# Shared expert, second group: four chunks of all four tiles' down products first, the last chunk and the half chunk behind them

## The chip, the cores and the metric

The kernel runs on one core of a Trainium2 chip. The metric is the device time of one execution in microseconds (us); the median of several runs is compared.

## The reference

The program is one transformer block for 2 sequences of 1024 tokens of width 512, all in float32. Ahead of the part that matters here stand a modulation from a small matrix product, two layer norms, and an attention whose keys and values are summed over the sequence, so that each sequence has one mixed output matrix. Then a mixture of experts follows; every token has two of eight routed experts, and all tokens go through one shared expert:

```python
x = hidden_states.reshape(-1, d)
scores = softmax(x @ gate_w)
topk_w, topk_idx = top_k(scores, 2)
...
g = silu(einsum('td,edh->teh', x, w_gate)) * einsum('td,edh->teh', x, w_up)
routed = einsum('teh,ehd,te->td', g, w_down, comb)
shared = silu(x @ sw_gate) * (x @ sw_up) @ sw_down
out = routed + shared
```

The shared expert has a hidden width of 704: five chunks of 128 and a half chunk of 64. The block's result is the residual plus a gate row `gb` times `out`.

## The kernel before

The 2048 tokens are 16 tiles of 128, in four groups of four tiles (one group has 512 tokens). Group 0's shared expert is worked out during the attention. Group 1's comes right behind the routing, ahead of the routed experts; that is the place of the change. Groups 2 and 3 come at the very end.

**Hidden units of group 1.** For each of five chunks n, `seven` (L1105) makes seven products of half-size operands on the tensor engine (PE, L1123) into PSUM banks: m1 and m2 into one of the two `start` banks, m6 and m7 into an `out` bank, m5 and m3 (tile m53) into an `mm` bank, m4 into one of the two `tr` banks. The scalar engine (ACT) copies m1 (L1131), and the vector engine (DVE) adds the others one after the other: L1133 to L1135, L1138 (m5), L1139 (m3), L1140 (m4), L1141. ACT then takes the sigmoid into `gT[:, n, :]` (L1143) and DVE multiplies twice (L1144, L1145); with L1145 chunk n of gT is ready. The half chunk, number 5, was made ahead of the five by `half_up`; its even tiles lie in partitions 0 to 63 and its odd ones in 64 to 127, so that two products with it run on the two halves of the array at the same time. DVE also works out the tables of experts (`expert_tables`, behind chunk 2) and of rows (`choice_rows`, L893 to L907, behind chunk 4).

**Down products of group 1.** `shared_down` (L1023) multiplies, for each tile j0 to j3 of the group, the six pieces of gT (stationary) with the six pieces of the down weights (128x512, moving) and sums them in one PSUM bank (L1031, names `sd`). A 128x512 product in float32 stands as two records in the trace. `down_ps` hands the four tiles the banks tr, tr, start, start. The weights lie in tiles `wd_s0a` (chunks 0 to 2) and `wd_s1a` (chunks 3, 4 and the half). A scheduler orders each engine's instructions from priorities and dependences. On PE it put j0's chunks 0 to 3, then j1's chunk 0, then j0's chunk 4, and then j1's chunks 1 to 4 and the two half chunks; behind them j2's five chunks, j3's five and their half chunks.

**Eviction.** `keep_shared` (L1149) is called for two tiles at a time: DVE multiplies the bank with `gb` into a row of the room `spare` (L1153), and GpSimd (POOL) adds that row to the residual tile (L1154). `spare` has two rows in turn here.

**What follows: the first pair of blocks.** `pair_sums` makes four sums of the first pair's expert weights on DVE, in this order: L1609 (s1), L1611 (s3), L1610 (s2), L1612 (s4). They are placed by `tc.issue_after` behind j1's eviction. `pair_in` (L1574) transposes two tiles of gathered rows `hp` on PE (L344, `tr_p`) into the two `tr` banks, and ACT copies them to `hpT` (L1578). `Pair` makes four sums of these rows on DVE (L1594 to L1597) into the room `token_sums`, which is the same memory as `spare`. `pair_hidden` then makes seven products per pair on PE (L1629): m1 and m2 read `hpT` and weights alone, m6 reads token_sums (L1595) and s2, and the others follow. From there PE goes through nine pairs and the single blocks to the last groups of the shared expert.

**SP's queue** issues the loads: the rows and weights of the pairs (L1556, L976 to L982), and the first parts of the shared gate and up weights once more (`s_again`, L1441). The down weights of the second pair, `wd_p` (L978, L982), take the room of `wd_s0a` and wait until that was read for the last time.

```python
for _ in shared_down(1, gTs[1], wds, keep_shared, down_ps()):
    pass
...
with tc.issue_after(kept_shared[5].ins):
    for step in steps:
        step()
pair_of = {0: Pair(pair_in(0, hps.pop(0)), token_rooms[:, 0])}
```

Of the kernel before, what the change touches and what calls it, by code (L numbers as in the profile page):

```python
# [18 lines left out]
P = 128  # L19
# [5 lines left out]
def kernel(  # L25
# [20 lines left out]
    nc = tc.nc  # L46
    B, S, D = x.shape
    E, _, H = w_gate.shape
# [8 lines left out]
    NF = HS // P  # L57
    HP = P // 2
# [567 lines left out]
    rows = const.tile([P, NT, TOPK], I32, name="rows")  # L626
# [257 lines left out]
    def choice_rows():  # L884

        pk = picks.rearrange("p t s e -> p (t s) e")
        rf = rowf.rearrange("p t s -> p (t s)")

        room = Carved(choice_room[:, NT * TOPK * E :])

        def by_choice(v, name):
            prod = Carved(choice_room).tile([P, NT * TOPK, E], FP, name=f"prod_{name}")
            nc.vector.tensor_mul(prod, pk, v.unsqueeze(1).to_broadcast([P, NT * TOPK, E]))  # L893
            t = room.tile([P, NT * TOPK], FP, name=f"of_{name}")
            nc.vector.tensor_reduce(t, prod, AX.X, ALU.add)
            return t

        beyond = by_choice(choice_of["ends"], "ends")
        nc.vector.tensor_tensor(beyond, rf, beyond, ALU.is_ge)
        shift = by_choice(choice_of["by_pair"], "pair")  # L900
        other = by_choice(choice_of["by_block"], "block")
        nc.vector.tensor_scalar(other, other, float(Y0), None, ALU.add)
        nc.vector.tensor_sub(other, other, shift)
        nc.vector.tensor_mul(other, other, beyond)
        nc.vector.tensor_add(rf, rf, shift)
        nc.vector.tensor_add(rf, rf, other)
        nc.vector.tensor_copy(yrows.rearrange("p t s -> p (t s)"), rf)  # L907


    gTs = {}  # L910
# [21 lines left out]
    def shared_chunk(n, g, wt):  # L932

        if n == 0:
            gTs[g] = gtp.tile([P, NF + 1, 512], FP, tag="gT", name=f"gT_{g}")
        pss = []
        for i, w in enumerate(wt):
            ps = sh_ps(f"p{i}_{n}_{g}")
            for k in range(KC):
                nc.tensor.matmul(  # L940
                    ps, w[:, k, :], hT[g][:, k, :], start=(k == 0), stop=(k == KC - 1)
                )
            pss.append(ps)
        sgm = unit.tile([P, 512], FP, tag="sg", bufs=2, name=f"sg_{n}_{g}")
        if n < NF:
            gate_full(gTs[g][:, n, :], sgm, *pss)
        else:
            gate_half(gTs[g], sgm, pss[0])

    def chunk_weights(n):  # L950
        def fetch(w, c0, src, h0, m):
            nc.sync.dma_start(
                w[:, :, c0 : c0 + m],
                src[:, h0 : h0 + m].rearrange("(k p) h -> p k h", p=P),
            )

        a = unit.tile([P, KC, P], FP, tag="wg", bufs=2, name=f"cg_{n}")
        if n == NF:
            fetch(a, 0, sw_gate, n * P, HP)
            fetch(a, HP, sw_up, n * P, HP)  # L960
            return (a,)
        u = unit.tile([P, KC, P], FP, tag="wu", bufs=2, name=f"cu_{n}")
        fetch(a, 0, sw_gate, n * P, P)
        fetch(u, 0, sw_up, n * P, P)
        return a, u
# [37 lines left out]
    def shared_weights():  # L1003

        tiles = [weight_tiles(f"s{i}a") for i in range(2)]
        wgu = []
        for i, (wg, wu, wd) in enumerate(tiles):
            views = []
            for w, src in ((wg, sw_gate), (wu, sw_up)):
                v = w.rearrange("p k h -> p (k h)").rearrange("p (k h) -> p k h", k=KH)  # L1010
                nc.sync.dma_start(
                    v, src.rearrange("(k p) h -> p k h", p=P)[:, i * KH : (i + 1) * KH, :]
                )
                views.append(v)
            wgu.append(views)
        wds = load_down([wd for _, _, wd in tiles])

        def up_part(which, i, h0, m):
            return wgu[i][which][:, :, h0 : h0 + m]

        return up_part, wds

    def shared_down(g, gT, wds, use, ps_of, apart=False):  # L1023


        for j0 in range(0, 4, 2):
            pss = [ps_of(f"sd_{g}_{j0 + i}") for i in range(2)]

            def chunk(i, c):
                rows = slice(i * HP, (i + 1) * HP) if c == NF else slice(0, P)  # L1030
                nc.tensor.matmul(  # L1031
                    pss[i],
                    gT[rows, c, (j0 + i) * P : (j0 + i + 1) * P],
                    wds[c][rows, :],
                    start=(c == 0),
                    stop=(c == NF),
                )

            if apart and j0 == 2:
                for i in range(2):  # L1040
                    for c in range(NF + 1):
                        chunk(i, c)
            else:
                for i in range(2):
                    for c in range(NF):
                        chunk(i, c)
                    if i == 0:
                        yield
                for i in range(2):
                    chunk(i, NF)  # L1050
            for i in range(2):
                use(g * 4 + j0 + i, pss[i])
            yield
# [51 lines left out]
    def seven(n, g, weights, b, behind=None):  # L1105


        a11, a12, a22, s1, s2, s3, s4 = weights
        c1, c2 = (
            gpool.tile([P, 2 * TH], FP, tag="sg", bufs=8, name=f"c{i}_{n}_{g}")  # L1110
            for i in range(2)
        )
        (c11, c12), (c21, c22) = ((c[:, 0:TH], c[:, TH:]) for c in (c1, c2))

        def products(ps, *pairs):
            halves = []
            for i, (w, h) in enumerate(pairs):
                half = ps[:, i * TH : (i + 1) * TH]
                with ExitStack() as order:
                    if behind:  # L1120
                        order.enter_context(tc.issue_after(behind.ins))
                    for k in range(KH):
                        nc.tensor.matmul(  # L1123
                            half, w[:, k, :], h[:, k, :], start=(k == 0), stop=(k == KH - 1)
                        )
                halves.append(half)
            return halves

        add = nc.vector.tensor_add
        m1, m2 = products(start_ps(f"m12_{n}_{g}"), (a11, b.b11), (a12, b.b21))  # L1130
        nc.scalar.copy(c11, m1)  # L1131
        m6, m7 = products(out_ps(f"m67_{n}_{g}"), (s2, b.t2), (s3, b.t3))
        add(c12, c11, m6)  # L1133
        add(c11, c11, m2)
        add(c22, c12, m7)  # L1135
        m5, m3 = products(mm_ps(f"m53_{n}_{g}"), (s1, b.t1), (s4, b.b22))
        (m4,) = products(tr_ps(f"m4_{n}_{g}"), (a22, b.t4))
        add(c12, c12, m5)  # L1138
        add(c12, c12, m3)  # L1139
        add(c21, c22, m4)  # L1140
        add(c22, c22, m5)  # L1141
        dst = gTs[g][:, n, :]
        on_act = nc.scalar.activation(dst, c1, AF.Sigmoid)  # L1143
        nc.vector.tensor_mul(dst, dst, c1)  # L1144
        return on_act, nc.vector.tensor_mul(dst, dst, c2)  # L1145

    kept_shared = {}

    def keep_shared(t, ps):  # L1149
# [110 lines left out]
    def chunk(n):  # L1260
        shared_chunk(n, 0, wts_c.pop(n))
        if n + 2 < NF + 1:
            wts_c[n + 2] = chunk_weights(n + 2)
# [111 lines left out]
    up_part, wds = shared_weights()  # L1375
# [43 lines left out]
    def down_ps():  # L1419

        turns = [tr_ps, tr_ps, start_ps, start_ps]

        def ps_of(name):
            turns.append(turns.pop(0))
            return turns[-1](name)

        return ps_of
# [102 lines left out]
    for n in range(NF):  # L1530
        _, after = seven(n, 1, ready.pop(n), toks[1])
# [4 lines left out]
                expert_tables(counts)  # L1536
    with tc.issue_after(after.ins):
        choice_rows()
    for _ in shared_down(1, gTs[1], wds, keep_shared, down_ps()):
        pass  # L1540


    def pair_value(row, j, most):
# [275 lines left out]
    for j in range(NPAIR):  # L1819
# [3 lines left out]
        else:  # L1823
            i = j + 2 - NPAIR
# [106 lines left out]
    up_part, wds = shared_again(firsts)  # L1931
# [107 lines left out]
```

## Time and profile before

| | |
|---|---|
| median of 3 runs | 765.99 us (765.92 to 766.53) |
| the profiled execution | 765.33 us |
| its span, first to last instruction | 763.6 us |
| tensor engine busy | 744.0 us, 97% of the span |
| vector engine busy | 497.3 us, 65% |
| granted TensorE clock, mean | 0.997 of full speed |
| down products of group 1, to the first transposes | 344.33 to 369.46 us of the span |

All times in rows of the trace are us from the span's start. A row of the timeline has the start, the length of the merged instructions, the engine, the source line, the operation and what it writes and reads; square brackets hold the idle time of the engine ahead of it and who ended that. Matmuls are pipelined: the end of a record lies some 0.16 us behind the start of the next one in a dense stream.

### The profile page before, as it was taken

To read this page: it belongs to the slowest core of one execution; us is meant where nothing else is said; L and a number is where in the kernel's file an instruction comes from. 1 tells how busy PE (TensorE), PEld (TensorE's weight loads), DVE (VectorE), ACT (ScalarE), POOL (GpSimd) and SP (SyncE) were. 2 spreads that over 40 slices of the span, in tenths; PEclk is the share of its full clock that TensorE was granted. 3 is DMA by queue.
4 is the path that set the end of the run, shared out by engine and by line. 5 is a ranking of instruction groups with operands and counts; after the bars stand their busy time and mean duration, and the time that the engine had idled before them with its cause. 6 is when DMAs were issued, how large, how long until landed. Compare 5 with 4: busy or idle time off the path is not lost. (4 is left out here: it accounts for less than half of the span.)

```text
span 763.6 us, 9423 instructions
## 1 busy us (share of the span) xinstructions
PE 744.0 (97%) x2941; PEld 439.5 (58%) x2941; DVE 497.3 (65%) x1211; ACT 239.3 (31%) x531; POOL 216.2 (28%) x243
## 2 busy tenths in 40 slices
PE   7999999999999999998999999999999999999997
PEld 2444444444444444683788878856656555788442
DVE  3899956898736888695677775623323222599864
ACT  4664523557643154110122222222221221122310
POOL 1234524863632687562100000000000000243630
PEclk9999999999999999999999999999999999999999
DMA  9950002312435711378846646669999984534551
GB/s 328 390 165 16 14 0 70 117 51 67 139 91 197 277 69 42 111 270 296 297 146 236 230 171 199 232 216 305 343 340 320 331 268 163 192 90 137 168 161 55
DMA packets 83413, 139.51 MB, mean 183 GB/s; under 512 B 7512, under 2 KB 41304, under 8 KB 83360
## 3 DMA queue, kind: packets, MB, share of 16 engines
q1 hardware_dynamic: 77024, 118.94, 45.6%
q0 software_dynamic: 5760, 18.88, 7.5%
q10 hardware_dynamic: 576, 1.05, 0.4%
q8 instruction: 25, 0.41, 0.2%
q14 instruction: 28, 0.23, 0.1%
HBM read 108.69 MB, written 30.16 MB: 182 GB/s over the span
## 5 line engine op out<-in xcount | busy, mean ns | idle before, releaser
L1490 POOL DMA_INDIRECT y<-ybuf,yrows x32 | 37.5, 1172 | 326.5 <-DVE c L1135 284.3
L417 PE MATMUL kv<-w_kv,xnT 128*128 128x512 f32 x256 | 115.2, 596 | 0.5 <-ACT xnT L400 0.5
L417 PEld LDWEIGHTS kv<-w_kv,xnT 128*128 128x128 f32 x256 | 46.9, 190 | 57.2 <-issue 49.5
L578 PE MATMUL o<-wp,xnT 128*128 128x512 f32 x128 | 57.3, 593 | 0.0
L1641 DVE TENSOR_TENSOR pc<-pc,m 128x256 f32<-128x256 f32 x63 | 26.0, 412 | 35.5 <-PE m L1629 35.3
L1685 PE MATMUL py<-wd_p,pgT 128*128 128x512 f32 (+1 forms) x108 | 48.1, 592 | 0.0
L1777 PE MATMUL by<-wd_r,gtT 128*128 128x512 f32 (+1 forms) x102 | 46.7, 594 | 1.1 <-ACTq L1911 1.1
L1744 PE MATMUL bg<-wg_r,hbT 128*128 128x352 f32 x136 | 43.2, 460 | 0.9 <-DVE gtT L1764 0.5
L1744 PE MATMUL bu<-wu_r,hbT 128*128 128x352 f32 x136 | 43.0, 459 | 0.0
L578 PEld LDWEIGHTS o<-wp,xnT 128*128 128x128 f32 x128 | 23.8, 190 | 28.6 <-issue 27.0
L1764 DVE COPY gtT<-gtr 128x256 f32<-128x256 f32 x17 | 7.2, 425 | 50.6 <-PE gtr L1756 50.6
L1629 PE MATMUL m<-token_sums,sums 128*128 128x128 f32 x324 | 37.5, 274 | 0.4 <-DVE token_sums L1595 0.4
L1629 PEld LDWEIGHTS m<-token_sums,sums 128*128 128x128 f32 x324 | 36.5, 182 | 1.1 <-DVE token_sums L1595 0.8
L1744 PEld LDWEIGHTS bu<-wu_r,hbT 128*128 128x128 f32 x136 | 25.8, 190 | 14.4
L447 POOL TENSOR_TENSOR cross<-kv 128x128 f32<-128x128 f32 x16 | 12.1, 758 | 74.1 <-DVE kv L424 42.4
L1744 PEld LDWEIGHTS bg<-wg_r,hbT 128*128 128x128 f32 x136 | 24.6, 190 | 12.7 <-ACT y L1781 1.4
L1685 PEld LDWEIGHTS py<-wd_p,pgT 128*128 128x128 f32 (+1 forms) x108 | 19.7, 190 | 21.1 <-issue 19.2
L1467 DVE TENSOR_TENSOR sg_b<-sg_b,bg 128x352 f32<-128x352 f32 x17 | 8.9, 521 | 34.6 <-ACT sg_b L1466 34.6
L1676 ACT ACTIVATE pgT<-pc 128x256 f32<-128x256 f32 (+1 forms) x36 | 11.1, 356 | 60.5 <-DVE pc L1641 60.5
L537 PE MATMUL wp<-aw,wqT 128*128 128x512 f32 x64 | 28.6, 597 | 0.9 <-DVE aw L518 0.7
L440 ACT ACTIVATE sq<-kv 128x512 f32<-128x512 f32 x32 | 20.2, 631 | 27.7 <-DVE kv L424 24.3
L617 POOL TENSOR_TENSOR hr<-hr,cb 128x512 f32<-128x512 f32 x16 | 22.3, 1392 | 21.3 <-issue 7.3
(371 smaller groups left out, 1542.3 us busy)
## 6 DMA issues: line engine op xcount, KB each, us to landing
wg_r<-in_w_gate_dram SPq DMA_DIRECT2D x17, 704.0 KB
wu_r<-in_w_up_dram SPq DMA_DIRECT2D x17, 704.0 KB
wd_r<-in_w_down_dram SPq DMA_DIRECT2D x17, 512.0 KB
wg_p<-in_w_gate_dram SPq DMA_DIRECT2D x9, 704.0 KB
wu_p<-in_w_up_dram SPq DMA_DIRECT2D x9, 704.0 KB
wmod<-in_wmod_dram SPq DMA_DIRECT2D x6, 1024.0 KB
wd_p<-in_w_down_dram SPq DMA_DIRECT2D x9, 512.0 KB
hp<-hbuf SPq DMA_DIRECT2D x18, 256.0 KB
```

The costliest lines, as they stand in the source:

```text
L417: nc.tensor.matmul(ps, xnT[g][:, k, j * P : (j + 1) * P], w_kv[:, i, k, :], start=(k == 0), stop=(k == KC - 1),)
L440: nc.scalar.activation(sq, kv[:, i, :], AF.Square, accum_out=ss[:, i : i + 1])
L447: nc.gpsimd.tensor_mul(cross[:, 0, :], pair[:, 0, :, 0], pair[:, 1, :, 1])
L537: nc.tensor.matmul(ps, wqT[:, k, f * P : (f + 1) * P], aw[:, k, :], start=(k == 0), stop=(k == KC - 1),)
L578: nc.tensor.matmul(ps, xnT[g][:, k, j * P : (j + 1) * P], wp[:, k, :], start=(k == 0), stop=(k == KC - 1),)
L617: nc.gpsimd.tensor_mul(h, h, cb1[b])
L1490: nc.gpsimd.indirect_dma_start(out=y, out_offset=None, in_=ybuf, in_offset=bass.IndirectOffsetOnAxis(ap=yrows[:, t, s : s + 1], axis=0), b ...
L1629: last[j] = nc.tensor.matmul(ps[:m, c * P : (c + 1) * P], a[:, k, h0 : h0 + m], h[:, k, :], start=(k == 0), stop=(k == KH - 1),)
L1641: op(*(t[:, 0:full] for t in tiles))
L1685: nc.tensor.matmul(ps, gT[:m, c, i * P : (i + 1) * P], w[2][:m, c, :], start=(c == 0), stop=(c == NH - 1),)
L1744: nc.tensor.matmul(ps[:, :H], hbT[:, k, :], wt[:, k, :], start=(k == 0), stop=(k == KC - 1))
L1777: nc.tensor.matmul(ps, gtT[:m, c, :], w[2][:m, c, :], start=(c == 0), stop=(c == NH - 1))
```

## The change

`shared_down` is replaced, for group 1 alone, by a new function. It takes the four banks at once, tr, start, start, tr for j0 to j3. It issues chunks 0 to 3 of all four tiles, then for j0 and j1 chunk 4 and the half chunk, with their evictions, and then the same for j2 and j3. No product is added or left out.

```diff
+    def shared_down_late(g, gT, wds, use):
+        pss = [
+            ps_of(f"sd_{g}_{j}") for j, ps_of in enumerate((tr_ps, start_ps, start_ps, tr_ps))
+        ]
+
+        def chunk(j, c):
+            i = j % 2
+            rows = slice(i * HP, (i + 1) * HP) if c == NF else slice(0, P)
+            nc.tensor.matmul(
+                pss[j],
+                gT[rows, c, j * P : (j + 1) * P],
+                wds[c][rows, :],
+                start=(c == 0),
+                stop=(c == NF),
+            )
+
+        for j in range(4):
+            for c in range(NF - 1):
+                chunk(j, c)
+        for j0 in range(0, 4, 2):
+            for c in range(NF - 1, NF + 1):
+                for i in range(2):
+                    chunk(j0 + i, c)
+            for i in range(2):
+                use(g * 4 + j0 + i, pss[j0 + i])
...
-    for _ in shared_down(1, gTs[1], wds, keep_shared, down_ps()):
-        pass
+    shared_down_late(1, gTs[1], wds, keep_shared)
```

As built, the order of other instructions changes in two places. On DVE the evictions of j2 and j3 (L1153) come ahead of the fourth weight sum (L1612) instead of behind it. On SP the two pieces of the second pair's `wd_p` come ahead of the second `s_again` load instead of behind it.

## The prediction

> **What bounds the kernel now.** I read the page first. The tensor engine (PE) is busy for nearly the whole span, and its clock row is flat.
>
> ```profile
> span 763.6 us, 9423 instructions
> PE 744.0 (97%) x2941; PEld 439.5 (58%) x2941; DVE 497.3 (65%) x1211; ACT 239.3 (31%) x531; POOL 216.2 (28%) x243
> ```
>
> So an edit gains only what it moves on PE. Next I read the timeline from the last mixed products (L1123) to the first pair's third product (L1629 out of token_sums). Columns: start, length in us, engine, line, operation; in brackets the idle time before it and who ended it.
>
> ```profile
> 342.60 1.03 PE L1123 MATMUL m<-hT,spare 128*128 128x256 f32 x4
> 343.46 1.03 PE L1123 MATMUL m<-mixed,wu_s1a 128*128 128x256 f32 x4
> 344.33 2.74 PE L1031 MATMUL sd<-wd_s0a,gT 128*128 128x512 f32 x6
> 347.99 0.42 DVE L1138 TENSOR_TENSOR c<-c,m 128x256 f32<-128x256 f32 x1 [3.23 <-remote]
> 349.45 0.42 DVE L1140 TENSOR_TENSOR c<-c,m 128x256 f32<-128x256 f32 x1 [1.04 <-remote]
> 349.93 1.12 PE L1031 MATMUL sd<-wd_s0a,gT 128*128 128x512 f32 x2 [2.00 <-DVE c L1140]
> 352.37 1.98 PE L1031 MATMUL sd<-wd_s1a,gT 128*128 128x512 f32 x2 [1.32 <-DVE gT L1145]
> 359.62 2.84 PE L1031 MATMUL sd<-wd_s0a,gT 128*128 128x512 f32 x6
> 359.79 1.29 DVE L1153 TENSOR_TENSOR spare<-sd,gb 128x512 f32<-128x512 f32 x2 [3.64 <-PE sd L1031]
> 360.57 3.13 POOL L1154 TENSOR_TENSOR x<-x,spare 128x512 f32<-128x512 f32 x2 [12.67 <-DVE spare L1153]
> 360.99 1.58 DVE L1609 TENSOR_TENSOR sums<-wu_p 128x704 f32<-128x704 f32 x1
> 362.50 1.95 DVE L1611 TENSOR_TENSOR sums<-wg_p,wu_p 128x704 f32<-128x704 f32 x1
> 364.37 0.88 DVE L1610 TENSOR_TENSOR sums<-sums,wg_p 128x704 f32<-128x704 f32 x1
> 369.46 1.09 PE L344 MATMUL tr_p<-ident,hp 128*128 128x128 f32 x8
> 369.63 1.29 DVE L1153 TENSOR_TENSOR spare<-sd,gb 128x512 f32<-128x512 f32 x2 [3.45 <-PE sd L1031]
> 370.40 2.50 POOL L1154 TENSOR_TENSOR x<-x,spare 128x512 f32<-128x512 f32 x2 [6.70 <-DVE spare L1153]
> 370.79 2.92 PE L1629 MATMUL m<-hpT,wg_p 128*128 128x128 f32 x24 [0.24 <-ACT hpT L1578]
> 372.93 0.43 DVE L1594 TENSOR_TENSOR token_sums<-hpT 128x256 f32<-128x256 f32 x1 [2.01 <-POOL x L1154]
> 374.08 4.26 PE L1629 MATMUL m<-token_sums,sums 128*128 128x128 f32 x36 [0.36 <-DVE token_sums L1595]
> ```
>
> PE pauses twice in the down products: for a PSUM bank of m4 (L1140) and for chunk 4 of gT (L1145). DVE is late because L1138 saw m53 done at 347.99, though its last product's record ends at 343.63. Last, stage windows (length, PE busy, clock, DMA share, GB/s):
>
> ```profile
> 345.67:349.08 3.41, 2.25 (x6) 1.00 1.02 386
> 349.08:352.50 3.42, 1.25 (x3) 1.00 1.03 408
> 352.50:355.90 3.40, 3.40 (x5) 0.50 0.39 119
> ```
>
> After the pauses PE runs 3.40 us at half clock, which loses 1.70 us. From 374.08 to the last product, PE shows no pause over 1.2 us and few over 0.2, none for a weight load, so what is won at 374.08 should arrive at the end. That start, called m6, is my meter.
>
> **The change, step by step**
>
> *PE's own stream.* Products j2 and j3 ran undisturbed from 359.62 to the first transpose at 369.46: 9.84 us for ten whole products and one pair of half chunks. Two such halves make 19.7 us. Before took 369.46 - 344.33 = 25.1, so 5.4 us are pauses, half clock and restarts. In the new order the bank of j1 and j2 are start banks, read long before; j3 takes m4's bank, wanted at 344.33 + 12 x 0.86 = 354.6 and free at 349.87; chunk 4 is wanted at 344.33 + 16 x 0.86 = 358.1 and ready at 352.32. Nothing waits: the stream ends at 344.33 + 19.7 = 364.0. This cover is 4.8 us for the bank and 5.8 us for the chunk.
>
> *Evictions of j0 and j1* come later: behind them stand two products (1.7) and a half pair (358.56 to 359.62, 1.1), so they are complete at about 361.1 instead of 359.6, and L1153 starts at 361.2, 1.4 later than before.
>
> *DVE's queue.* In the changed program's order L1609, L1611 and L1610 still stand between the evictions of j0/j1 and those of j2/j3; only L1612 moves behind. Shifted by 1.4: L1611 ends at 365.8 and L1610 at 366.65 (1.58 and 1.95 where POOL adds beside them; L1610 alone takes 0.88). L1153 of j2/j3 then runs to 367.9, although PE finished them at 364.0.
>
> *The new wait.* tr_p for the second half of the pair's rows takes j3's bank; before, both transposes had banks of j0 and j1. It stands in PE's order ahead of everything. The first transpose goes at 364.0 (0.5 us; its rows hp were issued from 353.6 on and landed by 357), the second at 367.95: a new PE pause of about 3.5 us. Behind it are m1 and m2, who wait for nothing else: 368.4 + 2.9 = 371.3.
>
> *m6* also needs token_sums, whose room is that of spare, so POOL must have added j3. POOL starts 0.77 after the eviction starts (366.6), at 367.4, and takes 2.50 alone or 3.13 beside a DVE sum; L1612 now runs beside its second half, so I take 2.8: 370.2, ends 369.9 and 370.5. L1594 to m6 took 1.15: m6 at 371.4 (between 371.3, where m2 ends, and 371.7). Gain 374.08 - 371.4 = 2.7 us, 2.4 to 2.8.
>
> *Moved on SP's queue:* the two pieces of wd_p (L978, L982) now go ahead of the second s_again load. They wait for the last read of wd_s0a, 366.78 before and about 357 now. Readers of both are pairs or blocks later; nothing added. Without that cover it would be 704 KB at 361 GB/s (this stretch's rate), 2 us. The instruction count is unchanged.
>
> *The clock.* A window of 3.41 us with 1.25 us of PE work was followed by half clock, one with 2.25 was not. The new pause of 3.5 us, if the window edges lie as in this execution (366.15 would be one), is cut in its middle and leaves about 1.7 us of work in each window: halfway between the two rows. If the edges lie otherwise, one window is emptier. A drop would cost between 0 and 1.7 us on m1 and m2, whose end is 0.1 us from deciding m6. I take none as the likeliest by a small margin, and price the drop as a rival.
>
> The Trainium skill speaks against the change here: "TensorE: Matmul & The Clock Gate", section "Why this matters for your kernels", wants no pause over about 3 us, since one idle window halves the clock. By that rule the old pauses (2.0 and 1.3 us) should have been free, and the trace shows that they were not; the new one would surely be punished, and the sum would be 2.7 less up to 1.7.
>
> **Sum.** The profiled execution took 765.33 us, span 763.6 and 1.7 around it; the median shown is 765.99, 0.66 above. 765.33 - 2.7 = 762.6 on its own scale, 763.3 on the median's, 763.2 to 763.6 by the bounds. 0.2% is 1.53 us.
>
> **Rivals**
>
> *Half clock behind the new pause.* Same steps, less 0.6 to 1.7 us: gain 1.0 to 2.1, time 763.9 to 765.0. For it: the pause is as long as a window. Against: 2.25 us of work did not trigger it.
>
> *The late signal follows PE's queue.* m53's completion reached DVE at 347.99, just as PE's eight down records ended at 347.92. If it comes only when PE runs dry, PE now runs on to j3 at 354.6, DVE gets m4 about 1.5 us later (349.45 - 347.99), j3 starts at 356.6: 2.0 us of the gain go, 0.7 stay, 765.3. Against: m4's signal came 1.5 us after PE was dry already.
>
> *Slower: the late signal comes again, on j0 and j1.* Their evictions now lead the whole chain to m6 (three sums, two evictions, POOL). The delay was 4.4 us (343.63 to 347.99) and 5.0 (344.49 to 349.45). It decides from 2.7 us on; at full size 1.7 to 2.3 slower, 767.7 to 768.3. Against: both evictions before started 0.2 us behind their products.
>
> *No stall outside this profile.* If plain runs had no late signal, before would have m6 at 374.08 - 5.4 = 368.7 and the new wait costs 2.7: 768.7. Against: plain runs took 765.92 to 766.53, not 5 us less than the profiled one.
>
> **How the numbers follow.** Sum as worked out 0.42; half clock 0.32; signal bound to the queue 0.09; late signal on j0/j1 0.11; no stall 0.06. The first three hold 0.83, and reach from 763.2 to 765.3; L1609 and L1611 ran 0.70 and 1.07 over the 0.88 of L1610; were the smaller excess to vanish, the low end would be 763.2 - 0.7 = 762.5. The high end is 765.3 with the 0.3 between the sum's 2.7 and its bound 2.4: 765.6. Over 0.2% faster means below 764.46: the first case and half of the second, 0.58. Within 0.2%: the other half and the third, 0.25. Slower: the last two, 0.17.
>
> **What would show it.** Right: down products from 344.3 to 364.0 without a pause; clock 1.00 at 352.5 to 355.9; a PE pause of 3 to 4 us ahead of the second tr_p, ended by DVE spare; L1594 released by POOL near 370.2; m6 near 371.4; all later lines moved by the same amount. Wrong: a pause inside the down products, a 0.50 window behind 366, m6 later than 372.5, or a weight load that PE waits for further on.

## The result and the profile after

| | before | after |
|---|---|---|
| median of 12 runs each | 766.51 us (763.26 to 768.08) | 769.42 us (766.17 to 771.31) |
| ratio | | 1.0041, 95% interval 1.0023 to 1.0058 |
| the profiled execution | 765.33 us | 769.84 us |
| down products, first one to first transpose (the front) | 25.13 us | 21.38 us, begun 3.00 us late |
| first transpose to m6 (the back) | 4.62 us | 8.69 us |

The change made the kernel slower by 0.4%, where 0.35% faster was forecast (763.3 us). The shares of the page hardly move: TensorE (PE) is busy 745.5 us of a span of 768.2. The loss is in one place, which the timeline of the changed kernel shows. Its lines read as before (rows of other engines and merged rows in between are left out); L1157 is the new down product, L1181 the eviction, L1182 the add on GpSimd (POOL), L1636, L1638 and L1637 are the weight sums, L1621 is the first sum of token_sums, L1656 the first pair's products.

```profile
344.67 1.03 PE L1123 MATMUL m<-mixed,wu_s1a 128*128 128x256 f32 x4
...
348.70 4.13 PE L1157 MATMUL sd<-wd_s0a,gT 128*128 128x512 f32 x6 [3.00 <-DVE choice_room L835]
...
363.38 6.77 PE L1157 MATMUL sd<-wd_s1a,gT 128*128 128x512 f32 x18
367.27 1.29 DVE L1181 TENSOR_TENSOR spare<-sd,gb 128x512 f32<-128x512 f32 x2 [8.15 <-PE sd L1157]
368.48 1.58 DVE L1636 TENSOR_TENSOR sums<-wu_p 128x704 f32<-128x704 f32 x1
369.99 1.95 DVE L1638 TENSOR_TENSOR sums<-wg_p,wu_p 128x704 f32<-128x704 f32 x1
370.08 0.66 PE L344 MATMUL tr_p<-ident,hp 128*128 128x128 f32 x4
371.86 0.88 DVE L1637 TENSOR_TENSOR sums<-sums,wg_p 128x704 f32<-128x704 f32 x1
372.66 1.28 DVE L1181 TENSOR_TENSOR spare<-sd,gb 128x512 f32<-128x512 f32 x2
373.42 3.15 POOL L1182 TENSOR_TENSOR x<-x,spare 128x512 f32<-128x512 f32 x2 [2.24 <-DVE spare L1181]
374.00 1.12 PE L344 MATMUL tr_p<-ident,hp 128*128 128x128 f32 x4 [3.26 <-DVE spare L1181]
374.90 4.03 PE L1656 MATMUL m<-hpT,wg_p 128*128 128x128 f32 x24
376.60 0.43 DVE L1621 TENSOR_TENSOR token_sums<-hpT 128x256 f32<-128x256 f32 x1 [1.17 <-POOL x L1182]
378.77 4.15 PE L1656 MATMUL m<-token_sums,sums 128*128 128x128 f32 x36
```

Two things are to be seen. First, the products run from 348.70 to 370.08 without a pause, so the two waits of before are gone; but PE stands idle for 3.00 us ahead of the first product, and the first ones run at half clock. Second, behind the products there is the new wait: j3 ended at 370.08 and its eviction ran at 372.66, behind three weight sums; the second transposes wait 3.26 us for it, m1 and m2 follow, slower than before (4.03 us against 2.92), and m6 starts 8.69 us behind the first transpose.

The windows of the clock (length, PE busy, clock, DMA share, GB/s) show why m1 and m2 are slow:

```profile
346.69:350.10 3.41, 1.40 (x4) 1.00 1.04 344
350.10:353.52 3.42, 3.42 (x6) 0.50 1.03 393
370.58:374.00 3.42, 0.16 (x3) 1.00 0.50 183
374.00:377.41 3.41, 3.41 (x16) 0.50 0.27 79
```

The new pause nearly fills one window (0.16 us of work), and the next one runs at half clock. The lateness of m6 against before, 378.77 - 374.08 = 4.69, stays to the end (4.5 to 4.6 us at the later lines); 0.62 of it stood already at the first transpose.

### The profile page after: what moved, and what is told of

Read it like the earlier page. It is cut to its first block, busy times and chain, and to the rows that moved or that the text cites. A ratio compares the mean times of both kernels' runs of the same rounds, so it can differ in the third digit from the quotient of the medians.

```text
span 768.2 us, 9425 instructions
## 1 busy us (share of the span) xinstructions
PE 745.5 (97%) x2941; PEld 441.5 (57%) x2941; DVE 497.9 (65%) x1211; ACT 239.1 (31%) x531; POOL 216.9 (28%) x243
## 5 line engine op out<-in xcount | busy, mean ns | idle before, releaser
L1656 PE MATMUL m<-token_sums,sums 128*128 128x128 f32 x324 | 37.4, 274 | 0.0
L1656 PEld LDWEIGHTS m<-token_sums,sums 128*128 128x128 f32 x324 | 36.5, 182 | 0.5 <-DVE token_sums L1622 0.2
L1712 PEld LDWEIGHTS py<-wd_p,pgT 128*128 128x128 f32 (+1 forms) x108 | 19.7, 190 | 21.1 <-issue 19.2
L1656 PEld LDWEIGHTS m<-hpT,wg_p 128*128 128x128 f32 (+1 forms) x216 | 26.3, 190 | 3.8 <-issue 3.4
```

Source lines behind the costliest of these rows:

```text
L1656: last[j] = nc.tensor.matmul(ps[:m, c * P : (c + 1) * P], a[:, k, h0 : h0 + m], h[:, k, :], start=(k == 0), stop=(k == KH - 1),)
L1712: nc.tensor.matmul(ps, gT[:m, c, i * P : (i + 1) * P], w[2][:m, c, :], start=(c == 0), stop=(c == NH - 1),)
```

## The experiments

I compare fronts and backs, as defined in the table. A single total says little here, since single runs of most of these kernels spread over 3 to 8 us. All ratios are to the kernel before on the same chip, with 95% intervals. Later edits are named once and combined.

**e1_before_again: the kernel before, a second profile.**

> The kernel before once more, for a second profile. Two stretches are read: the front, from the first down product of the group to the first transpose (before 369.46 - 344.33 = 25.1 us, after 370.08 - 344.67 = 25.4 with the late start of the products), and the back, from the first transpose to m6 (before 374.08 - 369.46 = 4.6, after 378.77 - 370.08 = 8.7). Theory (the stall is chance, the new wait is not): the back is 4.6 +- 0.2 again, and the front lies anywhere from 19.7 (no pause) to 26. Rival (the stall belongs to the old order): the front is 25 +- 1 again, with the pauses at L1140 and L1145 and the half clock in the same places. Time within 0.2% of the kernel before in both.

Measured: 766.57 us, ratio 1.0015 (0.9994 to 1.0036); back 4.62 again. The front was 22.99 behind a first product that came 1.59 us late, and the pauses were others: 0.80, 0.39 and 1.32 us, with no half clock. Here L1133 of an earlier chunk started late, at 334.76 (idle 3.42 us for its product), where before had L1138 late at 347.99. So the back is fixed and the stall at the front changes its form from execution to execution; its size, late start counted, was nearly the same.

**e2_bank: j3 in an mm bank.**

```diff
- enumerate((tr_ps, start_ps, start_ps, tr_ps))
+ enumerate((tr_ps, start_ps, start_ps, mm_ps))
```

> The changed kernel with j3's bank out of the mm pair instead of the tr pair: the second four transposes wait for no eviction of j3, and nothing else moves. Theory (the vector engine's queue decides, the bank is only the first to show it): no pause ahead of the second transposes, but m6 still waits for token_sums, whose room is free only when POOL has added j3, and j3 is still evicted behind three weight sums. By the rows of after (first transpose 370.08, POOL done about 376.57, L1622 ended 377.70) the back is 7.7, the pause stands between m2 and m6, time 768.0 to 769.5. Rival (the bank alone is the new wait): back 4.6, time 765.0 to 766.0.

Measured: 768.60 us, ratio 1.0043 (1.0016 to 1.0070); front 19.58, back 7.67, the figure expected. Timeline of e2:

```profile
348.03 0.42 DVE L1138 TENSOR_TENSOR c<-c,m 128x256 f32<-128x256 f32 x1 [3.04 <-remote]
349.47 0.42 DVE L1140 TENSOR_TENSOR c<-c,m 128x256 f32<-128x256 f32 x1 [1.02 <-remote]
...
364.47 1.09 PE L344 MATMUL tr_p<-ident,hp 128*128 128x128 f32 x8
...
372.14 5.90 PE L1656 MATMUL m<-token_sums,sums 128*128 128x128 f32 x36 [3.41 <-DVE token_sums L1622]
```

The transposes no longer wait, and nothing is won: the pause, 3.41 us now, moves behind m2, because token_sums waits for POOL, POOL for j3's eviction, and that for the weight sums. The bank was only the first wait to end late. By chance this execution has the very stall of the profile of before (L1138 at 348.03 against 347.99, L1140 at 349.47 against 349.45), and in the new order it costs PE nothing. Against 25.13 us the front of 19.58 is the full forecast gain.

**e3_sums_ahead and e4_both: the weight sums ahead of the evictions, with the tr bank and with the mm bank.**

```diff
- with tc.issue_after(kept_shared[5].ins):
+ with tc.issue_after(after.ins):      # after: L1145 of chunk 4
      for step in steps:
```

> The changed kernel with the four weight sums of the first pair placed on the vector engine beside choice_rows (idle there from 358.9 to 367.3 in the profile after), ahead of all four evictions; j3 keeps its tr bank. Theory: j2 and j3 are evicted directly behind their last product, 1.5 us after the first transpose could start, so the pause ahead of the second transposes shrinks from 3.3 to about 1.0; m1 and m2 end at 1.5 + 0.5 + 0.24 + 2.92 = 5.2 and the back is 5.2 instead of 8.7, no half clock; time 3 to 4 us under after's, 765.3 to 766.5. Rival (the order of the products itself costs, as all four tiles finish within 5 us of each other): back over 7, time over 768.

> Both: j3 in an mm bank and the weight sums ahead of the evictions. Theory: transposes, m1, m2 and m6 follow as before, back 4.6, no pause over 0.6; the front is that of the new order. If the new order saves something at the front on average, the time is below before's by that: after's loss of 2.9 us against an added back of 4.1 leaves 1.2, so 765.3. Rival (the old order's stall of 5.4 us is regular and the new order takes it away): 761 to 762.5. Rival (the product order gains nothing at all): 766.5.

Measured: e3 763.36 us, ratio 0.9975 (0.9952 to 0.9998), back 4.67; e4 763.45 us, ratio 0.9976 (0.9952 to 1.0000), back 4.62. Timeline of e3:

```profile
368.62 0.66 PE L344 MATMUL tr_p<-ident,hp 128*128 128x128 f32 x4
370.13 0.66 PE L344 MATMUL tr_p<-ident,hp 128*128 128x128 f32 x4 [0.86 <-DVE spare L1181]
...
373.28 4.21 PE L1656 MATMUL m<-token_sums,sums 128*128 128x128 f32 x36
```

With the sums out of the way j3 is evicted at once, the pause falls from 3.26 to 0.86 us, and the whole 4 us of the back are gone, with either bank. The new order with this one more edit is under before by 2.5 us in both, by the medians, more than I had expected (0 to 1.2 for e3, 1.2 for e4); the interval of e3 only just leaves out no change, and that of e4 ends at it. My expectation for e3 was 0.5 us too high at the back: the second transposes went at 1.51 as expected, but the copy's 0.24 us did not show, and m1 and m2 take 2.66 us from start to start, not the 2.92 of the merged row. In both executions the first product was late again (1.60 and 2.99 us).

**e5_sums_alone: the same edit in the old order.**

> The kernel before, old product order, with the four weight sums ahead beside choice_rows, as in e3. Theory (the saving of e3 is that of the product order at the front, and the sums only keep the back short): back 4.6, which was not late for the sums before either, front as before, time within 0.2% of before. Rival (the saving of e3 comes from the place of the sums): 0.3% under before, as e3.

Measured: 766.67 us, ratio 1.0005 (0.9991 to 1.0018); front 24.67, back 4.62. The place of the sums by itself is worth nothing, so the saving of e3 is that of the product order.

**e6_zeros_early and e7_zeros_early_new: what makes the signals late?** DVE and ACT start late behind PE products whose records ended 3 to 5 us earlier. In 334 to 350 us the transfers are near saturation (DMA share 0.92 to 1.02 in before), and POOL issues eight scatters of zero rows. e6 takes 2 MB of other zero stores out of the stage.

```diff
+ zeros_e = hrow.tile([P, D], FP, tag="hr", name="zeros_e")    # near 115 us
+ ... the stores of zeros to hbuf (one) and ybuf (seven)
- the same eight stores in block_table (334 to 338 us)
```

> The kernel before with the eight plain stores of zeros (seven to ybuf, one to hbuf, 2 MB) issued near 115 us, where the transfers are light, instead of 334 to 338 us; the eight scatters of zeros by GpSimd stay. Theory of the late signals (all engines' signals are late while the transfers are saturated, 380 to 420 GB/s from 334 us on): the transfers of the stage end some 5 us earlier, no signal is over 1 us late after 340, the front falls from 25 to 20 to 22 and the time by 2 to 4 us. Rival (the signals are late while GpSimd issues scatters): they stay as late as before, in the same places relative to the scatters, and the time is within 0.3% of before.

> The changed kernel with the sums ahead (e3) and the zeros early (e6). Theory (the new product order saves only what late signals cost): if e6 loses the late signals, this is level with e6 within 0.3%; if e6 keeps them, this is 2 to 3 us under e6. Rival (the new order saves something of its own): 2 to 3 us under e6 in both cases.

Measured: e6 769.82 us, ratio 1.0044 (1.0029 to 1.0059); e7 768.44, 1.0025 (1.0016 to 1.0034). The theory of saturated transfers fell: the DMA share from 334 to 350 us was 0.08 to 0.51 now, and the time rose where it should have fallen. The rival did not foresee the time either (0.3% at most). The zero stores gone, POOL ran its zero scatters from 334.38 on, right behind the ones before, and the late signals moved with them (L1130, the same operation as L1133, at 346.52 behind 3.93 us of idle time). PE's own products even paused 0.3 to 0.7 us in 340 to 346, and the down products started at 351.86. At nearly the same backs (4.62 and 4.67) the new order of e7 had a front of 19.68 against 21.76; its time is 1.4 us under e6, where 2 to 3 was expected.

**e8_zero_rows_sp: the zero rows stored by SP's queue.**

```diff
- scatter(endi[:, e : e + 1], zeros_t)          # GpSimd's queue
+ r = nc.values_load(endi[0:1, e : e + 1], engines=[SP], ...)
+ nc.sync.dma_start(hbuf[bass.ds(r, P), :], zeros_t)
```

> The kernel before with the eight scatters of zero rows (128 rows each, GpSimd's queue, 338 to 348 us) put as eight plain stores at a row read from endi on SP's queue; the bytes are the same. Rival of the late signals (GpSimd's scatters): no late signal from 338 us on, front 20 to 22 us and the time 2 to 4 us under before; those at 330 to 334 us stay. Theory (saturated transfers): signals stay late, time within 0.3%, or above since the first pair's weights are issued 3 us later behind eight more stores.

Measured: 763.11 us, ratio 0.9953 (0.9937 to 0.9968); front 21.77, back 4.63. The bytes are the same, the transfers from 338 to 346 us run no slower (311 to 357 GB/s, before 270 to 328), and from 335 us to the evictions DVE waited for no PE product over 0.6 us; the late one at 333.54, beside the scatters that remain, stayed (2.77 us). What is left at the front is mainly one pause of 1.32 us for chunk 4. The edit takes away both GpSimd's issuing and its indirect transfers; which of the two delays the signals was not separated.

**e9_after_again and e10_new_zero_rows_sp: the changed kernel a second time, and with the zero rows on SP.**

> The changed kernel once more, for a second profile. Theory (the new wait is fixed by the vector engine's order): pause of 3.0 to 3.4 us ahead of the second four transposes, back 8.2 to 8.8 in any execution; the front lies between 19.6 and 21.5 behind a start that is 0 to 3 us late. Rival (the back of 8.7 was chance as well): back under 7. Time 0.2 to 0.6% over before.

> The changed kernel with the eight stores of zero rows on SP's queue as in e8, where no signal was late from 335 us on. Theory: the front loses what e8 still paused for chunk 4 (21.77 to about 19.7), the back is 8.2 to 8.8 as before, so this is 4.1 - 2.1 = 2 us slower than e8: about 765. Rival (with the late signals gone the changed order is level with or under e8): 763 or less.

Measured: e9 766.04 us, ratio 1.0039 (1.0016 to 1.0062), front 19.62, back 8.71; e10 764.65 us, ratio 1.0000 (0.9984 to 1.0015), front 19.58, back 8.71. Timeline of e9:

```profile
368.59 0.66 PE L344 MATMUL tr_p<-ident,hp 128*128 128x128 f32 x4 [3.26 <-DVE spare L1181]
```

The pause is 3.26 us in both, to the hundredth as in the first profile; a half clock stands behind each. The cost is fixed, as DVE's queue is.

**e11_new_sums_sp: new order, sums ahead, zero rows on SP.**

> The changed kernel with the sums ahead (e3) and the zero rows on SP (e8): the version that should beat both. Theory: front 19.7 to 20.5, back 4.7, no pause over 1 us; e8 less the 2.1 us at its front less the rest of its clock loss: 761 to 761.7, 0.6% under before. Rival (the new order has nothing left to save once the signals are on time): 763, level with e8.

Measured: 760.54 us, ratio 0.9948 (0.9929 to 0.9967), front 19.61, back 4.67. It beats both kernels. By its ratio it was no better than e8, by its time 2.6 us better; the chips differed, so these were run once more on one.

**e12_old_sp, e13_new_sp, e14_new_sums_sp: the three on one chip.**

> The old order with the zero rows on SP (e8 again), for a comparison on one chip with the next two. Front 21.0 to 22, of which 1.3 is the pause for chunk 4; back 4.6; time 0.4 to 0.5% under before. This is the base of the three.

> The new order with the zero rows on SP (e10 again). Theory (the new order then saves the 2.1 us of the front and pays 4.1 at the back): 2 us over e12. Rival (half clock behind the new pause counts in full): 3 to 4 us over e12.

> The new order with the sums ahead and the zero rows on SP (e11 again). Theory: 2.0 us under e12, for its front of 19.6 against 21.8 at equal backs. Rival (nothing left to save): level with e12 within 0.5 us.

| | time us | front | back | forecast to e12 | measured to e12 |
|---|---|---|---|---|---|
| e12, old order | 763.07 | 21.77 | 4.62 | | |
| e13, new order | 764.98 | 19.64 | 8.71 | +2 | +1.9 |
| e14, new order, sums ahead | 761.10 | 19.63 | 4.67 | -2.0 | -2.0 |

Ratios to before: 0.9981 (0.9957 to 1.0004), 0.9997 (0.9981 to 1.0014), 0.9949 (0.9931 to 0.9967). For e12 0.4 to 0.5% under before was forecast; it is 0.2%, and its interval includes no change. Its own time is that of e8 (763.07 and 763.11), but the median of before beside it was lower (765.50 against 766.73). With the signals on time the sum closes: e13 has 2.13 less at the front and 4.09 more at the back, 1.96 in all, and 1.9 was measured. What the new order saves by itself is this line of e12, the wait for chunk 4, and the slower restart around it:

```profile
352.66 1.12 PE L1040 MATMUL sd<-wd_s1a,gT 128*128 128x512 f32 x2 [1.32 <-DVE gT L1154]
```

e12 also tells more of the late start of the first down product. DVE was held up early in e12 as well, about as long as in after (3.54 us against 3.42; L1142 of e12 is the same operation as L1133):

```profile
334.53 0.42 DVE L1142 TENSOR_TENSOR c<-c,m 128x256 f32<-128x256 f32 x1 [3.54 <-PE m L1132]
```

Yet its first down product started only 0.2 us late. In the profiles with a late start (after, e1, e3, e4) DVE waited again from 344 to 349 us, beside the zero scatters, 0.2 to 1.2 us at a time, and the product started 0.5 to 0.8 us behind the end of the L1140 that frees its bank; in e12 these waits are gone and that distance is 0.06 us. None of the six profiles with the zero rows on SP (e8, e10 to e14) has a start over 0.22 us late, so the late start seems to need the zero scatters as well.

**e15_scatters_twice: the zero scatters doubled, in the kernel before.**

```diff
- for e in range(E):
+ for e in [*range(E), *range(E)]:
      scatter(endi[:, e : e + 1], zeros_t)
```

> The kernel before with each of the eight scatters of zero rows issued twice (same rows, same zeros), so that GpSimd issues scatters until about 358 us instead of 348. Theory (signals are late while GpSimd issues scatters): late signals of the vector engine and pauses of TensorE of 1 to 3 us go on in 350 to 358, front 25 to 29 us, time 1 to 4 us over before. Rival (the scatters are beside the point): front as before, time within 0.2%, apart from hp's rows, which may land later.

Measured: 768.99 us (763.0 to 776.9), ratio 1.0031 (1.0000 to 1.0063); front 30.19, back 4.62. Timeline of e15:

```profile
345.93 1.03 PE L1123 MATMUL m<-mixed,wu_s1a 128*128 128x256 f32 x4
...
352.69 0.42 DVE L1138 TENSOR_TENSOR c<-c,m 128x256 f32<-128x256 f32 x1 [5.44 <-remote]
...
357.08 0.98 POOL L632 DMA_INDIRECT hbuf<-zeros_t,endi  x1 [0.30 <-issue]
357.68 0.42 DVE L1140 TENSOR_TENSOR c<-c,m 128x256 f32<-128x256 f32 x1 [4.57 <-remote]
358.15 2.08 PE L1031 MATMUL sd<-wd_s0a,gT 128*128 128x512 f32 x2 [7.76 <-issue]
```

m4's last product ended by its record at 346.96, and DVE acts on it at 357.68, 10.7 us later, with scatters still being issued (they end at 360.7). PE stands still for 7.76 us, and the clock is halved for 10.2 us; the front is over the 25 to 29 us that I expected. The interval of the times reaches down to no change, and the profiled execution (772.78 us) is one of the slowest, so it is this trace and not the median that shows the effect. Removed, the scatters take the late signals with them (from 335 us on); doubled, they lengthen them.

## Why the prediction was wrong

**Steps that held.** The stream without pauses was put at 19.7 us: the executions without a late start show 19.58 to 19.64. The covers of j3's bank and of chunk 4 held even in e2, with the worst stall. DVE's order, the three sums at 1.58, 1.95 and 0.88, and the new wait of the second transposes (3.5 forecast, 3.26 measured) came as described. No weight load was waited for, and the moved transfers on SP's queue cost nothing that a later line shows.

**The back was too short by 1.3 us.** Forecast from the first transpose, m6 stood at 371.4 - 364.0 = 7.4; it is 8.7. Two terms. POOL's adds take 3.15 us beside L1639, not the 2.8 that I took between 2.50 and 3.13: token_sums is ready 7.62 behind the first transpose (L1622 ended at 377.70), and e2, where only this counts, has 7.67. The other 1.0 is the half clock, priced at 0.6 to 1.7 as a rival and put under the main case "by a small margin". The pause was not cut in its middle: the windows before the drop had 0.16, 0.86 and 0.71 us of work (after, e9, e2), and the five profiles with a pause of 3.26 or 3.41 us here (after, e2, e9, e10, e13) all show it. The rule of the Trainium skill's "TensorE: Matmul & The Clock Gate", section "Why this matters for your kernels", against pauses over about 3 us, was right about this pause, and I overruled it with one row.

**The front was the larger error.** The step that failed is the 5.4 us: a stall seen in one execution, taken as what the new order removes in every execution, with the first down product starting on time. The stall has two forms. In one (before, e2, e5) m53 and m4 of the last chunk reach DVE late; there the new order saves up to 5.5 us (25.13 and 24.67 against 19.58). In the other (after, e1, e3, e4) DVE is held up two chunks earlier and again from 344 us on, so that the first down product itself starts late, which no order of the products mends. e9 shows neither. Counted from the time at which the last hidden product leaves PE free, the old order took 25.1, 24.7 and 24.7 us (before, e1, e5), the new one 24.5, 19.6, 22.5, 24.4 and 19.6 (after, e2, e3, e4, e9): 2.7 saved in the mean. And 18 of the 119 runs of before that stood beside the experiments took 760.2 to 761.8 us, some 5 us under the medians, with none between 761.8 and 762.5. Such runs most likely had no stall, though no profile caught one. The prediction gave the rival "no stall outside this profile" 0.06 on the ground that three plain runs took 766; three runs could not show this.

**The sum with measured terms.** 2.7 saved at the front, 4.1 lost at the back: 1.4 us slower. Measured: 2.9, interval 1.8 to 4.4. The sign and the cost at the back are settled; 1.5 us remain between eight profiles with chance stalls and the medians. By form, the same terms give 3.8 slower with the late start of after (24.5) and 1.1 faster without (19.6), so the median hangs on how often each occurs. The two profiles of the new order without a late start, e2 and e9, are the fastest of their twelve runs (764.95 and 764.45, medians 768.60 and 766.04), which speaks for the late start being the commoner form there; no run counted them. Without the late signals nothing remains (e12 to e14).

**The rivals.** "Half clock behind the new pause" came true. "The late signal comes again, on j0 and j1" did not: in e9 these evictions started 361.87 - 345.05 = 16.8 us behind the first product, the 16.9 of the forecast (361.2 - 344.33). "Bound to PE's queue" fell with e2, where DVE had m53 at 348.03 while PE ran on until 364.5.

## What to carry to other kernels

Before a stall is counted as gain, find what makes it, or see it in a second profile: here its cause was not only the order that the edit changed, but another engine's scatters, and moving those (0.5% under before in e8, 0.2% in e12) was worth about as much as the mended edit (e3, 0.25%). An edit that brings the end of several tiles together must also look at what stands in the evicting engine's queue between them; the gain came when the weight sums moved, not when the bank did. And a pause about as long as a clock window should be priced with the half clock behind it.

## What the runs showed of the hardware

- While GpSimd issued indirect scatters (one each 1.28 us), completions of PE reached DVE and ACT 3 to 5 us late (10.7 in e15), in steps of about 1.5 us (347.99 and 349.45 before). PE too started late behind DVE: 0.5 to 0.8 us behind the end of L1140 in after, e1, e3 and e4, against 0.06 in e12 without the zero scatters. It was not so beside every scatter: from 321 to 328 us DVE started on time beside them, in before for instance at 323.88 behind 0.72 us of idle time. Why the one and not the other stays open; plain stores of the same bytes on SP's queue did not do it.
- The busy time of PE in a window does not alone decide the clock. In this stage windows with 1.69 us of work (350.69 to 354.10 in e5) or less were followed by half clock, while one with 1.82 (345.10 to 348.51 in e1) was not; near 97 us windows with 2.08 (after) and 2.27 (e1) were. What differs there was not tested.
